# Context tails loaded for two batches at once, a first tile transposed in two halves, and two steps set in another order

## The chip, the core and the metric

The kernel runs on one NeuronCore of one Trainium2 chip. The core has five engines with instruction queues of their own: PE (TensorE, matrix products and transposes through an identity matrix), DVE (VectorE), ACT (ScalarE), POOL (GpSimd) and SP (SyncE, which here only issues DMA transfers). Sixteen DMA engines move data between the chip's memory (HBM) and the core's working memory (SBUF); PE writes to eight accumulator banks (PSUM). The metric is the device time of one execution, in microseconds.

## What is computed

A block of three layers on `x` (8 batches of 64 rows, width 512), each behind a layer norm and added to `x`. All data is 32-bit floating point. The layer that the change touches most is the first, cross-attention from 64 rows of `x` to 1601 context rows per batch:

```python
qp = q @ Wq + bq
kp = k @ Wk + bk
vp = v @ Wv + bv
attn = softmax(qp @ kp.T / sqrt(512))     # k = v = ctx_1024, 1601 rows per batch
x = x + attn @ vp                          # q = layernorm(x)
...
x = x + attn_layer(layernorm(x))           # 16 heads of 32, sigmoid instead of softmax, gates
...
x = x + ffn(layernorm(x))                  # 8 experts, the best one per row
```

## The kernel before

The 512 rows of `x` are four tiles (0 to 3) of 128 rows; a tile holds two batches. For cross-attention the kernel never forms keys: it multiplies a tile's projected queries by Wk transposed (`keyed`), and takes the scores against the context itself. The values likewise: the probabilities multiply the context (`attend`), and the sum is projected by Wv afterwards (`at_out`). So each tile needs the 1601 context rows of its two batches twice: as they are, and transposed.

**Loads.** A batch's first 1536 rows come in three chunks of 1 MB (`load_group`, groups 0 to 2, issued at L216), the last 65 rows as a "tail" (group 3, L223): four loads of 17, 16, 16 and 16 rows that go to partitions 0, 32, 64 and 96 of a tile of their own, `tails[k][b2]`, two buffers for two batches. POOL clears these four tiles first (L205); the second and later of its memsets stand behind the one that begins the identity matrix, and the first stands between that matrix's two instructions. All large loads are issued by SP in program order unless the scheduler moves them: the first tile of `x`, half of Wq, the other three tiles of `x`, the other half of Wq, WkT in halves, then for tile 0 the chunks of groups 0, 1, 2 for both batches and the eight tail loads. An issue waits until the load eight places before it has landed, because eight completion semaphores go round.

**Transposes of the context.** DVE turns blocks of 32x32 (L245 for a chunk, L252 for a tail): `turn_group(T, p, q, b2, g)` makes group `g` of quarter `q` of the width for batch `b2` of tile `p`. For tile 0 seven of the eight blocks `T` are turned group by group as the chunks land (`turn_first`), the eighth, (3, 1), behind them.

**Order.** PE runs in exactly the program's order all through the kernel (a manual schedule); DVE and ACT do so in the first part, up to the scores of tile 0, and in some later stretches. The first part on PE is: idle transposes of the identity, the transposes of the first normalized tile (`turn_x(0)`, L179; one bank, copied to SBUF by ACT in two halves, L304), two idle transposes, `project_q` of tile 0 (L315, which goes through the four chunks of width in order), transposes of tiles 1 and 2, `keyed(0)`, `project_q` of tiles 1 to 3, the scores of quarter 0 of tile 0 over the first 256 columns (`scores(..., hi=256)`), a bias product (L379), the same scores over the remaining columns (`scores(..., lo=256)`, which need groups 2 and 3 of both batches), then quarters 1 to 3 (all L411).

After the scores of a tile follow its softmax on DVE and ACT (exponentials at L433 and L439), transposes of the probabilities (`chance`, L457), and `attend`. For tiles 1 to 3 the Wv projection of the tile before (`at_out`, L187 and the sum at L485) is issued with `chance` as a step between its two halves:

```python
            at_out(p - 1, chance)
            if p == 1:
                keep_keyed(NT - 1, qk)
```

The second layer and the experts are written as a list of named steps whose order is PE's order. Near the end one such list has `flip(0)` (transposes of the first sorted rows, L179, copied by ACT at L1087; the rows were written to memory by POOL and come back by a load that SP issues at L1083), `split(2)` (transposes of queries and keys of tile 2, copied by ACT and DVE, L561 and L563) and `up_first(0)` (the first expert product, L1097, which needs the copy that `flip(0)` makes).

Of the kernel before, what the change touches and what calls it, by code (L numbers as in the profile page):

```python
# [10 lines left out]
F32 = mybir.dt.float32  # L11
# [6 lines left out]
P = 128  # L18
B, S, D = 8, 64, 512
SK = 1601  # L20
NT = B * S // P
DC = D // P
# [14 lines left out]
def perceiver_kernel(ctx: ExitStack, tc: tile.TileContext, out: bass.AP, t: dict):  # L37
# [13 lines left out]
    def slab(name):  # L51
        return slabs.tile([P, DC, D], F32, tag="slab", name=name)
# [10 lines left out]
    def bank4(name):  # L63
        return banks.tile([P, DC, P], F32, tag="bank", name=name)
# [8 lines left out]
    def load_x(i, n):  # L73
        rows = t["x"].rearrange("(i p) d -> p i d", p=P)
        nc.sync.dma_start(out=xall[:, i : i + n, :], in_=rows[:, i : i + n, :])
# [8 lines left out]
    for dc in (0, 2):  # L84
        nc.sync.dma_start(out=wq[:, dc : dc + 2, :], in_=t["xWq"][:, dc : dc + 2, :])
        if dc == 0:
            for i in range(1, NT):
                load_x(i, 1)
    wkT = slab("w_xWkT")
    for dc in (0, 2):  # L90
        nc.sync.dma_start(out=wkT[:, dc : dc + 2, :], in_=t["xWkT"][:, dc : dc + 2, :])
# [84 lines left out]
    def transposed(src, name):  # L176
        tp = bank4(f"t_{name}")
        for dc in range(DC):
            nc.tensor.transpose(tp[:, dc, :], src[:, dc * P : (dc + 1) * P], ident)  # L179
        return tp  # L180

    def projected(srcT, w, name, between=None):
# [14 lines left out]

    scale = 1.0 / math.sqrt(D)
    tails = [
        [one.tile([P, D], F32, tag=f"tail{k}{b2}", name=f"tail{k}{b2}") for b2 in range(2)]  # L200
        for k in range(2)
    ]
    for k in range(2):
        for b2 in range(2):
            nc.gpsimd.memset(tails[k][b2], 0.0)  # L205


    REST = (17, 16, 16, 16)
    def load_group(p, g):
        got = []  # L210
        for b2 in range(2):
            src = t["ctx"][2 * p + b2]
            if g < 3:
                c = slab(f"cx_{p}_{g}_{b2}")
                rows = src[: 12 * P, :].rearrange("(q c) d -> q c d", c=12)
                ins = nc.sync.dma_start(out=c, in_=rows[:, 4 * g : 4 * g + 4, :])  # L216
                if p == 1 and g == 0:
                    tc.keep_in_program_order(ins)
            else:
                c = tails[p % 2][b2]  # L220
                k0 = 12 * P
                for a, n in enumerate(REST):
                    ins = nc.sync.dma_start(  # L223
                        out=c[32 * a : 32 * a + n, :], in_=src[k0 : k0 + n, :]
                    )
                    if p < 2:
                        tc.keep_in_program_order(ins)
                    k0 += n
            got.append(c)
        return got  # L230

    cxs = {}
    for g in (0, 1, 2, 3):
        cxs[0, g] = load_group(0, g)


    NB = D // 32
# [60 lines left out]
        return xns  # L298

    def turn_x(i, xn):  # L300
        tp = transposed(xn, f"xn{i}")
        step = 2 if i == 0 else DC
        for dc in range(0, DC, step):
            nc.scalar.copy(  # L304
                xnT[:, dc : dc + step, i * P : (i + 1) * P], tp[:, dc : dc + step, :]
            )

    def project_q(i0, n, ps):

# [19 lines left out]
        T = slabs.tile([P, DC, D], F32, tag="slab", name=f"T_0_{q}_{b2}")  # L329
        first[q, b2] = T[:, :, :416]  # L330

    def turn_first(g, qs=range(4)):
        for b2 in range(2):
            for q in qs:
                if (q, b2) in first:
                    turn_group(first[q, b2], 0, q, b2, g)
# [29 lines left out]
    def keep_keyed(p, ps):  # L366
        n = len(ps)
        for k in range(n):
            qkTs[p + k] = row4(f"qkT{p + k}")
            for h in range(n):  # L370
                w = DC // n
                nc.scalar.copy(qkTs[p + k][:, h * w : h * w + w, :], ps[h][:, :, k, :])
# [521 lines left out]
    def at_out(i, between=None):  # L894
        project(i, tile_of[i]["acT"], between)
# [15 lines left out]
    def do(*steps):  # L911
        for f, i in steps:
            f(i)
# [29 lines left out]
            for q in qs:  # L943
                turn_group(second[q, b2], 1, q, b2, g)

    for qs in (range(2), range(2, 4)):
        for g in (2, 3):
            turn_first(g, qs)
    scores(0, 0, R, sc, [first[0, 0], first[0, 1]], lo=256)
    first[3, 1] = blocks(0, 3, 1)  # L950
    for q in range(1, 4):
# [7 lines left out]
    for p in range(NT):  # L959
        i = p - 2  # L960
        if p > 0:
            sc = [bank(f"sc_{p}_{a}") for a in range(4)]
        for q in range(4) if p > 0 else ():
            if p == 1 and q == 0:
                nTs = [second[1, 0], second[1, 1]]
            elif p == 1 and q == 1:
                turn_second(2, (2,), (0,))
                nTs = [second[2, 0], blocks(1, 2, 1)]
                turns.__exit__(None, None, None)
            else:  # L970
                nTs = quarter(p, q + 1) if q < 3 else None
            if i >= 0 and q == 3:
                scores(p, q, R, sc, Ts, range(3))
                do((back, i))
                scores(p, q, R, sc, Ts, (3,))
            else:
                scores(p, q, R, sc, Ts)
            Ts = nTs
            if i >= 0 and q < 3:
                do(((split, align, sums)[q], i))  # L980
        if p > 0:
            do((at_turn, p - 1))
        if p == 0:
            turns = tc.manual_schedule(engines={mybir.EngineType.DVE})
            turns.__enter__()
        L, over_sum = softmax(p, sc)
        pts = []
        if p == 0:
            second = {(q, b2): block_tile(1, q, b2) for q in range(2) for b2 in range(2)}
            for g in (0, 1, 3):  # L990
                turn_second(g)
        r = over_sum()
        acts = ExitStack()
        if p < NT - 1:
            acts.enter_context(tc.manual_schedule(engines={mybir.EngineType.Activation}))

        def chance():
            pts.append(chances(p, len(pts), L))

        if p == 0:  # L1000
            qk = keyed(1, 2)
        else:
            if i >= 0:
                do((output, i))
        if p == 0:
            chance()
            tables()
            keep_keyed(1, qk)
            R = queries(1)
        elif p + 1 < NT:  # L1010
            R = queries(p + 1)
            if p == 1:
                qk = keyed(NT - 1)
            at_out(p - 1, chance)
            if p == 1:
                keep_keyed(NT - 1, qk)
        else:
            at_out(p - 1, chance)
        if 0 < p < NT - 1:
            load_pair(p + 1)  # L1020
        if p == 1:
            blank_rows()
        ac = bank(f"ac_{p}")
        if i >= 0:
            do((face, i))
        for g in range(4):
            if g < 3:
                chance()
            if p == 0 and g == 3:
                turn_second(2, (0,), (0,))  # L1030
                second[2, 0] = block_tile(1, 2, 0)
                for gg in (0, 3, 1):
                    turn_second(gg, (2,), (0,))
            if p > 0 and g == 3:
                do((turn, p - 1))
            if 0 < p < NT - 1 and g > 0:
                deal_queries(R, qkTs[p + 1], g, range(2))
                deal_queries(R, qkTs[p + 1], g, range(2, 4), nc.gpsimd.tensor_copy)
            if i >= 0 and g == 1:
                do((gated, i))  # L1040
            if 0 < p < NT - 1 and g == 0:
                deal_queries(R, qkTs[p + 1], 0, range(2))
                deal_queries(R, qkTs[p + 1], 0, range(2, 4), nc.gpsimd.tensor_copy)
            attend(p, g, pts[g], ac)
            if p == 0 and g < 3:
                deal_queries(R, qkTs[p + 1], g)
                if g == 2:
                    deal_queries(R, qkTs[p + 1], 3)
            if p > 0 and g == 0:
                do((norm, p - 1))  # L1050
            if i >= 0 and g == 0:
                do((logits, i))
            if i >= 0 and g == 1:
                do((routed, i))
        if p == 0:
            turn_second(2, (0,), (1,))
        tile_of[p]["acs"] = divided(p, ac, r)
        if p == 0:
            turn_second(2, (1,))
        if 0 < p < NT - 1:  # L1060
            do((unit_q, p - 1))
        acts.close()
        if 0 < p < NT - 1:
            Ts = quarter(p + 1, 0)
            do((unit_k, p - 1), (gates, p - 1), (values, p - 1))
        elif p == 0:
            Ts = [second[0, 0], second[0, 1]]
# [78 lines left out]
    fetch(0)  # L1146
    load_experts_late(gu, dn)
    do((unit_q, 2), (at_turn, 3), (unit_k, 2), (at_out, 3), (norm, 3), (gates, 2))
    do((values, 2), (flip, 0), (split, 2), (up_first, 0), (turn, 3), (align, 2), (up_last, 0))
    do((unit_q, 3), (over, 0), (sums, 2))  # L1150
    unit_k(3, lambda: back(2))
    do((flip, 1), (output, 2))
# [134 lines left out]
```

## Time and profile before

| | us |
|---|---|
| three runs | 288.61, 288.14, 286.54 (median 288.14) |
| the profiled execution | 286.62 |
| its span, first to last instruction | 284.7 |
| PE idle at the start, up to the first idle transpose | 1.86 |
| PE idle from 30 to 33 us, two waits for DVE | 2.3 |
| DVE waiting for context chunks up to 70 us, seven waits | 14.4 |
| SP held in the tail issues of tile 0, first to last issue | 18.4 |
| mean of one chunk transpose on DVE (128x512) | 0.68 |
| DMA traffic, whole span | 57.72 MB, mean 203 GB/s |

The profile is one execution recorded by the hardware profiler. In its timeline a row is: start in us from the beginning of the span, duration, engine, line of the kernel, operation, the tile written and the tiles read, the shape, how many instructions are merged, and in brackets how long the engine stood idle before and what released it. PEld is the weight load of TensorE, SPq a transfer being issued by SyncE. The granted TensorE clock is full in all forty slices of the page. The trace also holds a record for each DMA packet and for each completion that a transfer posts; the prediction calls the latter landing records.

The waits that SP's queue had in the first 35 us, longest in total first:

```profile
SPq L223 <- DMA cx<-in_ctx_dram: 14.9, 6, 3.4
SPq L216 <- DVE T L252: 3.5, 1, 3.5
SPq L223 <- DMA w_xWkT<-in_xWkT_dram: 1.8, 2, 0.9
```

### The profile page before, as it was taken

The numbers are of one execution on the slowest core, as the hardware profiler recorded it, in microseconds if no ns is written. First come the engines' busy times: TensorE is split into PE (matmuls) and PEld (weight loads), VectorE is DVE, ScalarE is ACT, GpSimd is POOL, SyncE is SP. The second block draws the span as 40 slices with busy tenths as digits, with TensorE's granted clock in tenths as the row PEclk, the third lists the DMA queues.
The fourth block names the chain that finished last, engine by engine and source line by source line (L and its number), as shares of the span: only waits on it lengthen the run. The fifth ranks groups of instructions, "written<-read, shape, count | busy, mean of one in ns | idle before, by whom it ended". The sixth has DMA issues, their size and how long they took to land. (4 is left out here: it accounts for less than half of the span.)

```text
span 284.7 us, 6695 instructions
## 1 busy us (share of the span) xinstructions
PE 270.7 (95%) x2724; PEld 136.0 (48%) x2724; DVE 159.1 (56%) x422; ACT 113.4 (40%) x244; POOL 70.5 (25%) x120
## 2 busy tenths in 40 slices
PE   6999699999999999999999999999999999999990
PEld 5975548335643345644434564434444555442320
DVE  3576729359432987846688765631562476384130
ACT  2574006980176522267744047534326424130210
POOL 3351560000971004060220400031140041404211
PEclk9999999999999999999999999999999999999999
DMA  6997686399799980000897036299980200614501
GB/s 210 423 416 308 196 290 236 92 423 395 265 316 397 383 321 9 6 0 0 315 361 284 2 146 211 92 294 367 359 309 2 76 0 2 211 48 149 151 0 45
DMA packets 20177, 57.72 MB, mean 203 GB/s; under 512 B 2418, under 2 KB 10658, under 8 KB 16432
## 3 DMA queue, kind: packets, MB, share of 16 engines
q1 hardware_dynamic: 17568, 50.37, 48.2%
q0 software_dynamic: 2432, 6.89, 6.9%
q8 instruction: 23, 0.38, 0.6%
q14 instruction: 10, 0.08, 0.1%
q10 hardware_dynamic: 144, 0.00, 0.0%
HBM read 50.94 MB, written 6.84 MB: 203 GB/s over the span
## 5 line engine op out<-in xcount | busy, mean ns | idle before, releaser
L245 DVE STREAM_TRANSPOSE T<-cx 128x512 f32<-128x512 f32 x96 | 61.5, 678 | 19.0 <-DMA cx<-in_ctx_dram 18.6
L411 PE MATMUL sc<-T,R 32*64 32x400 f32 (+4 forms) x1088 | 48.1, 480 | 2.4 <-DVE T L252 2.3
L467 PE MATMUL ac<-cx,pt 128*64 128x512 f32 x192 | 43.8, 598 | 0.1
L411 PEld LDWEIGHTS sc<-T,R 32*64 32x64 f32 x1088 | 24.1, 131 | 21.0 <-issue 14.6
L401 ACT COPY R<-qkT 32x512 f32<-32x512 f32 x40 | 24.6, 616 | 0.7
L467 PEld LDWEIGHTS ac<-cx,pt 128*64 128x64 f32 x192 | 12.7, 136 | 22.2 <-issue 21.4
L1097 PE MATMUL gu<-wgu,xeT 128*32 128x512 f32 x192 | 22.8, 597 | 0.0
L544 POOL TENSOR_TENSOR gm_k<-qn_k,c_gk 128x512 f32<-128x512 f32 x4 | 5.1, 1282 | 60.0 <-DVE qn_k L539 60.0
L401 POOL COPY R<-qkT 32x512 f32<-32x512 f32 x24 | 14.5, 605 | 17.4 <-PE sc L411 10.9
L422 DVE TENSOR_REDUCE mx<-sc 128x1 f32<-128x400 f32 (+1 forms) x16 | 8.1, 568 | 13.5 <-PE sc L411 13.5
L187 PE MATMUL p_po<-w_xWv,acT 128*128 128x512 f32 x32 | 14.9, 592 | 0.0
L359 PE MATMUL qk<-qpT,w_xWkT 128*128 128x128 f32 (+1 forms) x96 | 14.8, 311 | 0.0
L187 PE MATMUL p_q<-w_aWq,xhT 128*128 128x512 f32 x32 | 14.8, 606 | 0.0
L187 PE MATMUL p_k<-w_aWk,xhT 128*128 128x512 f32 x32 | 14.7, 595 | 0.0
L315 PE MATMUL qp<-xnT,w_xWq 128*128 128x128 f32 (+1 forms) x64 | 14.5, 383 | 0.1
L187 PE MATMUL p_o<-w_aWo,cT 128*128 128x512 f32 x32 | 14.5, 596 | 0.0
L187 PE MATMUL p_v<-w_aWv,xvT 128*128 128x512 f32 x32 | 14.4, 592 | 0.0
L507 POOL TENSOR_TENSOR x<-x,c_bo 128x512 f32<-128x512 f32 x4 | 5.1, 1273 | 36.3 <-DVE xh L506 36.3
L359 PEld LDWEIGHTS qk<-qpT,w_xWkT 128*128 128x128 f32 x96 | 13.4, 191 | 1.4 <-issue 0.6
L459 ACT COPY pt<-pp 128x512 f32<-128x512 f32 (+1 forms) x16 | 8.2, 510 | 10.4 <-PE pp L457 10.3
L315 PEld LDWEIGHTS qp<-xnT,w_xWq 128*128 128x128 f32 x64 | 9.7, 191 | 4.5 <-ACT xnT L304 0.4
L1132 PE MATMUL y<-wd,hT 128*32 128x512 f32 x96 | 11.5, 596 | 0.3 <-ACT hT L1124 0.3
(197 smaller groups left out, 371.3 us busy)
## 6 DMA issues: line engine op xcount, KB each, us to landing
cx<-in_ctx_dram SPq DMA_DIRECT2D x24, 1024.0 KB, 8.5
wgu<-in_wgT_dram SPq DMA_DIRECT2D x8, 512.0 KB, 9.9
wgu<-in_wuT_dram SPq DMA_DIRECT2D x8, 512.0 KB, 7.1
wd<-in_wdT_dram SPq DMA_DIRECT2D x8, 512.0 KB
rd<-blank POOLq DMA_DIRECT2D x6, 258.0 KB, 6.1
in<-rd SPq DMA_DIRECT2D x6, 258.0 KB, 4.2
xd<-blank POOLq DMA_DIRECT2D x6, 256.0 KB, 5.8
in<-xd SPq DMA_DIRECT2D x6, 256.0 KB, 7.1
```

Of the source, the lines that this page charges most:

```text
L187: nc.tensor.matmul(ps, lhsT=srcT[:, dc, :], rhs=w[:, dc, :], start=(dc == 0), stop=(dc == DC - 1),)
L245: nc.vector.transpose(T[:, :, 128 * g : 128 * g + 128].rearrange("p b (c k) -> p b c k", k=32), cxs[p, g][b2][:, :, 128 * q : 128 * q + 12 ...
L315: nc.tensor.matmul(ps[ec][:, : n * P], lhsT=wq[:, dc, ec * P : (ec + 1) * P], rhs=xnT[:, dc, cols], start=(dc == 0), stop=(dc == DC - 1),)
L359: nc.tensor.matmul(ps[c * n // DC][:, c % (DC // n), :, :], lhsT=wkT[:, ec, c * P : (c + 1) * P], rhs=qpT[:, ec, cols], start=(ec == 0), s ...
L401: copy(R[32 * a : 32 * a + 32, j::4, :], qkT[32 * j : 32 * j + 32, :, :])
L411: nc.tensor.matmul(sc[a][r : r + S, lo : min(hi, WIDTH[a])], lhsT=R[32 * a : 32 * a + 32, b, r : r + S], rhs=Ts[b2][32 * a : 32 * a + 32, ...
L422: nc.vector.tensor_reduce(mx[:, a : a + 1], sc[a][:, : WIDTH[a]], AX.X, ALU.max)
L459: nc.scalar.copy(pt[:, :nch, :], tp[:, :nch, :])
L467: nc.tensor.matmul(ac[r : r + S, :], lhsT=pt[:, j, r : r + S], rhs=cx[b2][:, j, :] if g < 3 else cx[b2], start=(g == 0 and j == 0), stop=( ...
L507: nc.gpsimd.tensor_tensor(xs[i], xs[i], bo, ALU.add)
L1097: nc.tensor.matmul(ps[c, :], lhsT=xTs[k][:, dc, c], rhs=ffw[e][0][:, dc, :], start=(dc == 0), stop=(dc == DC - 1),)
L1132: nc.tensor.matmul(y[c, :], lhsT=hT[:, ic, c], rhs=ffw[e][1][:, ic, :], start=(ic == 0), stop=(ic == IC - 1),)
```

## The change

- The tails of two batches share one tile of 2x512 columns per partition, `tails[k]`, and come in four loads per tile of `x` instead of eight: each of the four takes its 17 or 16 rows of both batches. POOL's four memsets become two of twice the width.
- For tile 0 the four tail loads are issued before the last chunk (group 2, second batch) instead of behind it. DVE's later `turn_first` steps follow that order.
- The fourth tile of `x` is loaded behind the second half of Wq.
- The first tile's four transposes go to two banks, two each; ACT copies the first half, DVE the second.
- For tile 2, `chance` comes behind `at_out` and no longer between its halves. Tiles 1 and 3 keep the step between.
- `split(2)` comes before `flip(0)`.

```diff
-            for i in range(1, NT):
-                load_x(i, 1)
+            load_x(1, 1)
+            load_x(2, 1)
+    load_x(3, 1)
...
     tails = [
-        [one.tile([P, D], F32, tag=f"tail{k}{b2}", name=f"tail{k}{b2}") for b2 in range(2)]
-        for k in range(2)
+        one.tile([P, 2, D], F32, tag=f"tail{k}", name=f"tail{k}") for k in range(2)
     ]
...
+    def load_tails(p):
+
+        c = tails[p % 2]
+        k0 = 12 * P
+        for a, n in enumerate(REST):
+            ins = nc.sync.dma_start(
+                out=c[32 * a : 32 * a + n, :, :],
+                in_=t["ctx"][2 * p : 2 * p + 2, k0 : k0 + n, :].rearrange("b r d -> r b d"),
+            )
+            if p < 2:
+                tc.keep_in_program_order(ins)
+            k0 += n
+        return [c[:, b2, :] for b2 in range(2)]
...
-    for g in (0, 1, 2, 3):
+    for g in (0, 1):
         cxs[0, g] = load_group(0, g)
+    cxs[0, 2] = [load_chunks(0, 2, 0)]
+    cxs[0, 3] = load_group(0, 3)
+    cxs[0, 2].append(load_chunks(0, 2, 1))
...
     def turn_x(i, xn):
-        tp = transposed(xn, f"xn{i}")
-        step = 2 if i == 0 else DC
-        for dc in range(0, DC, step):
-            nc.scalar.copy(
-                xnT[:, dc : dc + step, i * P : (i + 1) * P], tp[:, dc : dc + step, :]
-            )
+        cols = slice(i * P, (i + 1) * P)
+        if i > 0:
+            nc.scalar.copy(xnT[:, :, cols], transposed(xn, f"xn{i}"))
+            return
+
+        for h, copy in enumerate((nc.scalar.copy, nc.vector.tensor_copy)):
+            tp = bank4(f"t_xn{i}_{h}")
+            for dc in (2 * h, 2 * h + 1):
+                nc.tensor.transpose(tp[:, dc, :], xn[:, dc * P : (dc + 1) * P], ident)
+            copy(xnT[:, 2 * h : 2 * h + 2, cols], tp[:, 2 * h : 2 * h + 2, :])
...
-    for qs in (range(2), range(2, 4)):
-        for g in (2, 3):
-            turn_first(g, qs)
+    turn_first(2, range(3), (0,))
+    turn_first(3, range(2))
+    turn_first(2, range(3), (1,))
+    turn_first(3, (2,))
+    for g in (2, 3):
+        turn_first(g, (3,))
...
-            at_out(p - 1, chance)
             if p == 1:
+                at_out(p - 1, chance)
                 keep_keyed(NT - 1, qk)
+            else:
+                at_out(p - 1)
+                chance()
...
-    do((values, 2), (flip, 0), (split, 2), (up_first, 0), (turn, 3), (align, 2), (up_last, 0))
+    do((values, 2), (split, 2), (flip, 0), (up_first, 0), (turn, 3), (align, 2), (up_last, 0))
```

More of the change, by code (lines that the diff above doesn't have):

```diff
@@ L199, in perceiver_kernel, with load_chunks @@
     tails = [
-        [one.tile([P, D], F32, tag=f"tail{k}{b2}", name=f"tail{k}{b2}") for b2 in range(2)]
-        for k in range(2)
+        one.tile([P, 2, D], F32, tag=f"tail{k}", name=f"tail{k}") for k in range(2)
     ]
     for k in range(2):
-        for b2 in range(2):
-            nc.gpsimd.memset(tails[k][b2], 0.0)
+        nc.gpsimd.memset(tails[k], 0.0)
     REST = (17, 16, 16, 16)
-    def load_group(p, g):
[L210 to L224, printed above, removed]
-                    )
[L226 to L230, printed above, removed]
+    def load_chunks(p, g, b2):
+        c = slab(f"cx_{p}_{g}_{b2}")
+        rows = t["ctx"][2 * p + b2][: 12 * P, :].rearrange("(q c) d -> q c d", c=12)
+        ins = nc.sync.dma_start(out=c, in_=rows[:, 4 * g : 4 * g + 4, :])
+        if p == 1 and g == 0:
+            tc.keep_in_program_order(ins)
+        return c
+    def load_tails(p):
[7 more added lines that the diff above has]
+            if p < 2:
+                tc.keep_in_program_order(ins)
+            k0 += n
+        return [c[:, b2, :] for b2 in range(2)]
+    def load_group(p, g):
+        return [load_chunks(p, g, b2) for b2 in range(2)] if g < 3 else load_tails(p)
     cxs = {}
-    for g in (0, 1, 2, 3):
+    for g in (0, 1):
         cxs[0, g] = load_group(0, g)
+    cxs[0, 2] = [load_chunks(0, 2, 0)]
+    cxs[0, 3] = load_group(0, 3)
+    cxs[0, 2].append(load_chunks(0, 2, 1))
     NB = D // 32
@@ L300, in turn_x @@
     def turn_x(i, xn):
-        tp = transposed(xn, f"xn{i}")
-        step = 2 if i == 0 else DC
-        for dc in range(0, DC, step):
-            nc.scalar.copy(
-                xnT[:, dc : dc + step, i * P : (i + 1) * P], tp[:, dc : dc + step, :]
-            )
+        cols = slice(i * P, (i + 1) * P)
[7 more added lines that the diff above has]
+            copy(xnT[:, 2 * h : 2 * h + 2, cols], tp[:, 2 * h : 2 * h + 2, :])
     def project_q(i0, n, ps):
@@ L330, in perceiver_kernel, with turn_first @@
         first[q, b2] = T[:, :, :416]
-    def turn_first(g, qs=range(4)):
-        for b2 in range(2):
+    def turn_first(g, qs=range(4), batches=range(2)):
+        for b2 in batches:
             for q in qs:
```

## The prediction

> **What bounds the kernel now.** The page's first part comes first: one engine fills the span.
>
> ```profile
> PE 270.7 (95%) x2724; PEld 136.0 (48%) x2724; DVE 159.1 (56%) x422; ACT 113.4 (40%) x244; POOL 70.5 (25%) x120
> ```
>
> PE is idle for 284.7 - 270.7 = 14.0 us; its timeline ends at 276.27 + 1.92 = 278.2, so 6.5 us of that is the last scatter behind it, and 7.5 us is all that a reordering can take back. The chain of waits helps little (it names only the last scatter), so the second view is the list of waits, for PE alone:
>
> ```profile
> PE sc L411 <- DVE T L252: 2.3, 2, 1.5
> PE idle L120 <- POOL ident masks.py:199: 1.9, 1, 1.9
> PE pp L457 <- ACT L L433: 0.8, 1, 0.8
> PE t_xe L179 <- DMA in<-xd: 0.6, 1, 0.6
> PE t_xn L179 <- DVE xn L288: 0.6, 1, 0.6
> ```
>
> The columns are total, times, longest. Four of these five rows lie at places that the diff touches; the third view, the timeline in order of time, shows each. The largest, around 24 to 33 us:
>
> ```profile
> 25.56 1.30 DVE L245 STREAM_TRANSPOSE T<-cx 128x512 f32<-128x512 f32 x2 [0.59 <-DMA cx<-in_ctx_dram]
> ...
> 28.48 1.08 PE L379 MATMUL qb<-qpT,c_xbk 128*32 128x128 f32 x32
> 28.74 1.31 DVE L245 STREAM_TRANSPOSE T<-cx 128x512 f32<-128x512 f32 x2 [1.88 <-DMA cx<-in_ctx_dram]
> ...
> 30.30 0.46 PE L411 MATMUL sc<-T,R 32*64 32x145 f32 x2 [0.74 <-DVE T L252]
> ...
> 31.90 0.51 DVE L252 STREAM_TRANSPOSE T<-tail 128x128 f32<-128x128 f32 x2 [1.47 <-DMA tail<-in_ctx_dram]
> 32.27 0.80 PEld L411 LDWEIGHTS sc<-T,R 32*64 32x64 f32 x49 [1.78 <-DVE T L252]
> 32.27 1.01 PE L411 MATMUL sc<-T,R 32*64 32x145 f32 x46 [1.52 <-DVE T L252]
> ```
>
> The last big chunk of each batch lands at 25.5 and 28.7; the second batch's tail only at 31.8. PE has done all else by 29.56 and takes up scores(lo=256) at 32.27; from there to 128 us it stands still for 0.2 us in all, so what is won at 32.27 stays won. The other two places, in PE's timeline:
>
> ```profile
> 125.99 1.88 PE L187 MATMUL p_po<-w_xWv,acT 128*128 128x512 f32 x4
> 128.63 0.65 PE L457 MATMUL pp<-ident,L 128*128 128x128 f32 x4 [0.75 <-ACT L L433]
> 129.12 1.88 PE L187 MATMUL p_po<-w_xWv,acT 128*128 128x512 f32 x4
> ```
>
> ```profile
> 209.70 0.63 PE L179 MATMUL t_xe<-ident,in 128*128 128x128 f32 x4 [0.64 <-DMA in<-xd]
> 210.16 0.60 PE L179 MATMUL t_q<-ident,qn_q 128*128 128x128 f32 x4
> 210.60 0.60 PE L179 MATMUL t_k<-ident,qn_k 128*128 128x128 f32 x4
> 211.13 2.06 PE L1097 MATMUL gu<-wgu,xeT 128*32 128x512 f32 x16
> ```
>
> **The change, part by part. First rows in halves.** Now four transposes start 5.88, 6.15, 6.36, 6.57, end 6.99, ACT copies at 7.03 and PE starts project_q at 7.46. With a bank per half ACT can start at the second transpose's end, 6.57, and is done by 6.57 + 0.03 + 0.37 = 6.97; but the two idle turns (6.79 and 7.00, 0.21 apart) stay ahead, so project_q starts at 7.21: 0.25 us. Its 17th matmul now waits for the second half of Wq (landed 9.27; 0.17 and 0.18 instead of 0.11 between starts there); with the fourth x tile behind it, one 0.67 us transfer less (x tiles 2 and 3 landed at 7.31 and 7.98), it lands at 8.6: 0.1 us more, 0.35 in all. DVE pays: its half of the copy (0.41, the row of the 128x256 hT copy) waits for the fourth transpose, so the statistics queued behind go from 6.68 to about 7.45, and xn1 to xn3 are each 0.75 later (9.8, 11.2, 11.9). PE wants xn2 at 11.1: 0.15 lost of the 0.35. POOL's tail memset ahead of the identity is twice as wide (0.53 becomes 0.96 by the 128x128 row, 0.21, and this one), so the idle turns begin at 2.3 instead of 1.86; their 3.2 us still end before xn0 at 5.82. All of this ends in the stall at 29.6 us: PE comes there 0.2 to 0.35 earlier and waits longer. I count it as nothing; if the stall went entirely it would be worth that much.
>
> The spacing of PE's matmuls drops from 213 to 112 ns at 7.7 us, with the idle turns begun at 1.86. The Trainium skill ("TensorE: Matmul & The Clock Gate", Part 1) has full clock after a free-running window of about 3.4 us with PE busy; by that rule a start 0.43 later risks, one time in eight, a further window at half rate, 1.7 us. In this trace the stall would swallow that too (from 29.2 to about 30.9).
>
> **The tails.** SP's eight tail issues now run from 10.6 to 29.05 us, the last held until the last big chunk has landed, 28.7 (eight completion semaphores go round). Afterwards four issues stand before that chunk; what they would wait for (x, WkT, the first chunk) lands by 14.6, and the chunk's own issue waits for one landing at 16.87. So SP is off the path and the DMA engines are on it. The landing records say how: a 16-row tail load leaves sixteen records, a 17-row one two, of which one is immediate; its rows go through one DMA engine, one after another (2 KB rows take 84 ns there, 8 KB rows of the chunks 313 ns). Both batches' 17 rows in one load leave 34 on that engine, and the last chunk's share now queues behind them. That engine finishes the previous chunk between 23.8 and 24.4 (fifteen of sixteen records), then 34 + 6 rows x 0.084 = 3.36, then 8 x 0.313 = 2.50: 29.7 to 30.2. Rows were slower, 149 ns, for half a microsecond around 26.5 when loads met; six such add 0.4, so 29.7 to 30.6, and I take 30.1. A second engine lags by 1.2 us since 16 us (25.54 for that chunk); with 6 rows and 2.50 it is done at 28.6, not last. DVE then needs one transpose, 0.71, and PE 0.06 after it: 30.1 + 0.8 = 30.9 instead of 32.27. **Gain 1.4** (0.9 to 1.8). DVE's reordered transposes fit: the first batch's and all tails' are done by 28.6, and behind the chunk it needs 0.67 for the next block of eight, while PE takes 4 us for scores(lo=256).
>
> The Trainium skill ("DMA: Bandwidth & Descriptors", "Why a DMA increments its semaphore by 16 and not by 1") gives a load the largest number of engines up to 16 that divides its slowest dimension: one for 17 rows, as the records show, and one again for 17x2. By that rule the change makes its one engine's queue longer ahead of the last chunk, and the sum above stands. The same page's rules for kernel authors say to coalesce small transfers since each pays about 2 us; by it four loads fewer would be worth 8 us, but consecutive 16-row loads land 0.17 us apart here, so they cost no such thing.
>
> Later tail loads (tiles 1 to 3) shrink to four issues each as well: PE waits for none of them now, so nothing.
>
> **at_out before chance, tile 2 only.** The pp transposes (L457) stand between two halves of a projection and wait for the exponentials, done about 128.5. Put behind, the second half (1.73 between starts) covers that: p_po runs 125.99 to 129.45, pp then, and the first attend, now at 131.80, comes 128.63 - 127.72 = 0.91 earlier, at 130.9 (0.75 by the idle column: a drain is counted busy). Its pt copy (ACT, 0.59 after pp ends at 130.05) is ready at 130.7: just in time. **Gain 0.8 to 0.9**, 0.7 if the copy is late.
>
> **split before flip.** t_xe waits for a landing at 209.6. Afterwards t_q and t_k (0.88) fill that time, t_xe runs from 209.8 to 210.4; but its copy (ACT, 0.59) had the two as cover, and up_first now waits for it: 210.42 + 0.59 + 0.05 = 211.06 against 211.13. The 0.64 stall becomes one of about 0.65 one step later: **0.1**. Where the landing is later than in this execution, up to 0.9 more. It follows PE: the stream ahead of it starts at 184.03 when PE frees a slab.
>
> Sum: 1.4 + 0.85 + 0.1 = 2.35. The profiled execution took 286.62 (span 284.7 and 1.9 around it), so 284.3 in its terms; it lies 1.5 under the median of the runs (286.54, 288.14, 288.61), and 288.14 - 2.35 = 285.8.
>
> **Rivals.** *Stall gone entirely*: the 34 rows spread over more engines, and the lagging one (28.6) is last: PE restarts at 29.4, gain 2.9, sum 3.8, 284.3. For it: half the issues; against: the two records of a 17-row load. *Given back*: tile 1's last chunk comes no earlier, and PE, which waits 0.19 at 71.87 for a block from it, waits longer there; only the two later parts stay: 0.95, 287.2. For it: DVE is idle 6.0 us before that chunk; against: its load (SP, 53.94) is held by PE's attend, so it moves along. *Slower*: one engine's queue, the 40 rows ahead of the last chunk, at the crowded price. Restart is 24.1 + 40r + 2.5 + 0.8; that equals 32.27 at r = 0.122 us, and eats the other 0.95 too at r = 0.145. At 0.16 (upper rows around 27 us) it is 33.8, 1.5 later, in sum 0.6 slower: 288.7. Against: 84 ns is the rule outside that half microsecond.
>
> **How the numbers follow.** Forecast 0.56, stall gone 0.20, given back 0.16, slower 0.08. The forecast's own bounds are gains of 1.6 (0.9 + 0.7) to 2.8 (1.8 + 0.9 + 0.1), so 285.3 to 286.5; runs differ by 2 us, so about 1 is added either way: 284.0 to 287.5 holds 8 in 10. One per cent, about what a measurement here tells from no change, is 2.9 us: over it lie stall gone and the forecast's upper end with the spread, 0.36; slower by that, 0.04; within, 0.60.
>
> **What would show it.** PE's restart of scores(lo=256) near 30.9 behind a T from cx rather than from tail; project_q at 7.2; no wait at pp of tile 2; t_xe's wait replaced by gu's for xeT. A restart past 32.3 proves the queue of one engine; one at 29.4 the spread; a new PE wait between 33 and 128 us, the giving back.

## The result and the profile after

The changed kernel takes 288.2 us (median of 17 runs, 286.44 to 290.19); the kernel before, run beside it, 286.81 (17 runs, 284.76 to 288.61). The ratio is 1.0064, with a 95% interval of 1.0037 to 1.0091: slower by 0.6%, where 0.8% faster was forecast, and above the top of the range, 287.5. A second set of runs of the same kernel (the fifth experiment) gave 1.0045 (1.0007 to 1.0083). The profiled execution of the changed kernel is the fastest of its 17, 286.44 us with a span of 284.3, so it shows where waits went, but not what a typical run costs.

The page's first part, and then the list of waits for PE (total, times, longest):

```profile
PE 270.9 (95%) x2724; PEld 137.1 (48%) x2724; DVE 159.5 (56%) x423; ACT 112.9 (40%) x243; POOL 70.2 (25%) x118
```

```profile
PE idle L121 <- POOL ident masks.py:199: 2.3, 1, 2.3
PE sc L420 <- DVE T L250: 2.2, 2, 2.0
PE gu L1112 <- ACT xeT L1102: 0.7, 1, 0.7
PE t_c L180 <- DVE cg L626: 0.5, 1, 0.5
PE sc L420 <- DVE T L257: 0.3, 1, 0.3
```

PE is busy for 270.9 us, before for 270.7. The wait at `pp` and the one of t_xe are gone, as forecast, and a new one of 0.7 for xeT has come. But the wait at the scores of tile 0 is not smaller. The timeline around it:

```profile
28.18 1.90 DVE L250 STREAM_TRANSPOSE T<-cx 128x512 f32<-128x512 f32 x3 [2.86 <-DMA cx<-in_ctx_dram]
...
29.01 1.08 PE L388 MATMUL qb<-qpT,c_xbk 128*32 128x128 f32 x32
30.03 0.89 DVE L257 STREAM_TRANSPOSE T<-tail 128x128 f32<-128x128 f32 x4
...
30.40 0.46 PE L420 MATMUL sc<-T,R 32*64 32x145 f32 x2 [0.30 <-DVE T L257]
...
32.09 1.30 DVE L250 STREAM_TRANSPOSE T<-cx 128x512 f32<-128x512 f32 x2 [1.18 <-DMA cx<-in_ctx_dram]
...
32.86 0.38 PE L420 MATMUL sc<-T,R 32*64 32x145 f32 x8 [2.01 <-DVE T L250]
```

PE is through with the bias product at 30.1 and has nothing to do, but for two products, until 32.86. The prediction had 30.9, the kernel before 32.27. The releaser is now a block from `cx`, the last chunk, as forecast. Its landing records run from 28.94 to 32.07, and the second-to-last chunk, which had ended at 25.54, now ends at 28.16. Both are later than in the sum, and not on one DMA engine alone: fifteen of the last chunk's sixteen shares are in at 31.25, where the sum had them at 28.6. The windows of 1 us of the kernel before, and under them those of the changed kernel, show why; the last two columns are the share of time in which the DMA engines were busy and what they moved:

```profile
core 0: us, PE busy (x) PEld busy (x) DVE busy (x) ACT busy (x) POOL busy (x), PEclk, DMA share, GB/s
...
24.00:25.00 1.00, 1.00 (x5) 0.60 (x4) 0.97 (x2) 0.58 (x1) 0.00 (x0) 1.00 1.00 418
25.00:26.00 1.00, 1.00 (x5) 0.60 (x4) 0.44 (x1) 0.00 (x0) 0.00 (x0) 1.00 0.99 408
26.00:27.00 1.00, 1.00 (x18) 0.42 (x25) 0.87 (x2) 0.33 (x1) 0.00 (x0) 1.00 0.70 185
27.00:28.00 1.00, 1.00 (x54) 0.86 (x42) 0.00 (x0) 0.25 (x1) 0.00 (x0) 1.00 0.12 39
```

```profile
24.00:25.00 1.00, 1.00 (x4) 0.57 (x3) 1.00 (x3) 0.37 (x1) 0.00 (x0) 1.00 0.99 211
25.00:26.00 1.00, 1.00 (x4) 0.57 (x3) 0.32 (x1) 0.21 (x1) 0.00 (x0) 1.00 0.96 186
26.00:27.00 1.00, 1.00 (x4) 0.38 (x2) 0.00 (x0) 0.00 (x0) 0.00 (x0) 1.00 1.17 203
27.00:28.00 1.00, 1.00 (x33) 0.79 (x40) 0.00 (x0) 0.58 (x1) 0.00 (x0) 1.00 0.86 207
```

Before, the chunk runs at 418 GB/s until it is through, and only then do the tail rows come, at 185 GB/s and less, with no chunk queued behind them. After, the DMA engines are as busy from 24 to 28 us as they were before from 24 to 26, but move 186 to 211 GB/s: rows and chunk packets run side by side. By the packet records that start from 24 to 28 us, an 8 KB packet of a chunk takes 0.614 us (median; 0.313 before), a 2 KB row 0.172 (0.094 before). In the three other traces of this order of loads (experiments 3, 5 and 10) the 8 KB packets take 0.39 to 0.41 in the same stretch, so 0.614 is the worst of four.

The two late steps, in PE's timeline:

```profile
126.72 3.60 PE L188 MATMUL p_po<-w_xWv,acT 128*128 128x512 f32 x8
130.16 0.60 PE L466 MATMUL pp<-ident,L 128*128 128x128 f32 x4
...
131.56 2.80 PE L476 MATMUL ac<-cx,pt 128*64 128x512 f32 x12
```

```profile
209.09 0.60 PE L180 MATMUL t_k<-ident,qn_k 128*128 128x128 f32 x4
209.52 0.60 PE L180 MATMUL t_xe<-ident,in 128*128 128x128 f32 x4
210.80 2.11 PE L1112 MATMUL gu<-wgu,xeT 128*32 128x512 f32 x16 [0.68 <-ACT xeT L1102]
```

Before, `pp` waited 0.75 between two halves of p_po, and the first attend was this row:

```profile
131.80 3.65 PE L467 MATMUL ac<-cx,pt 128*64 128x512 f32 x16
```

Now the eight products run through and the first attend starts at 131.56, although PE had come to this place 0.73 later (126.72 against 125.99). That is 0.97 won. At 209.52 t_xe no longer waits, and gu waits 0.68 one step later: the trade of 0.1 that was forecast.

In the tables below the mean granted clock of a run is used, since the runs of most kernels fall into two groups by it. Runs far above the others of their kernel are left out, as in the ratios; with them the shares of runs at 0.990 and below in the last table would be 36 of 105 and 22 of 29, and not 30 of 96 and 21 of 28.

### The profile page after: what moved, and what is told of

The parts are those of the page before. It is cut to its first block, busy times and chain, and to the rows that moved or that the text cites. A ratio compares the mean times of both kernels' runs of the same rounds, so it can differ in the third digit from the quotient of the medians.

```text
span 284.3 us, 6663 instructions
## 1 busy us (share of the span) xinstructions
PE 270.9 (95%) x2724; PEld 137.1 (48%) x2724; DVE 159.5 (56%) x423; ACT 112.9 (40%) x243; POOL 70.2 (25%) x118
```

## The experiments

Two theories stood first. **Queue**: the rows of the early tails slow the last two chunks. **Clock**: the longer idle stretch of PE lets its clock drop. A rival was that the late steps cost time. The call `idle_turns(n)`, which some of the kernels add, transposes the identity n times on PE and uses the result nowhere.

**1. Tails behind the last chunk again** (changed kernel, VectorE's order of before).

```diff
-    for g in (0, 1):
+    for g in (0, 1, 2, 3):
         cxs[0, g] = load_group(0, g)
-    cxs[0, 2] = [load_chunks(0, 2, 0)]
-    cxs[0, 3] = load_group(0, 3)
-    cxs[0, 2].append(load_chunks(0, 2, 1))
...
```

> The changed kernel with the four merged tail loads of tile 0 issued behind the last chunk again, and DVE's turn_first steps in the order of before. Theory queue (the 34 rows on one DMA engine, and the crowding while they mix with chunk packets, make the last chunk late: 32.07 us in the changed kernel): the last chunk lands near 28, its packets take 0.31 us again, the tails are in by 30.4 to 31, scores(lo=256) restart at 31.0 to 31.6 instead of 32.86, and the time is 1.3 to 1.8 us under the changed kernel's by that alone. Theory clock (a PE stall of over 2 us in one piece lets the granted clock drop to half for a window of about 3.4 us, at a cost of up to 1.7 us in most executions): the stall is shorter and broken up, the drop becomes rarer, another 0.5 to 1.5 us go. Rival late steps (the loss lies in the p = 2 or flip order): no change against the changed kernel.

Measured: 286.51 us, ratio 0.9985 (0.9945 to 1.0024). The last chunk lands from 26.22 to 29.89 (near 28 was expected), the tails by 31.02, PE restarts at 31.61:

```profile
31.61 5.63 PE L417 MATMUL sc<-T,R 32*64 32x145 f32 x128 [2.35 <-DVE T L254]
```

The loss is gone when the order of loads and of VectorE's transposes goes, so it lies in that order; the restart is still no earlier than 31, since the rows land late instead. (The products take 5.63 us here because the granted clock is at half behind the wait, see below.)

**2. The 17-row load as 16 rows and 1** (changed kernel).

```diff
-        for a, n in enumerate(REST):
...
-                out=c[32 * a : 32 * a + n, :, :],
...
+        for a, n in enumerate(REST):
+            for r0, m in ((0, 16), (16, n - 16)):
+                if m:
...
+                        out=c[32 * a + r0 : 32 * a + r0 + m, :, :],
...
```

> The changed kernel with every 17-row tail load cut in 16 rows and 1 row. Theory queue in its first form (one engine works off 34 rows alone): the tails take half a microsecond on all engines, the last chunk lands at 28.5 to 29, scores(lo=256) restart at 29.4 to 29.8, and the time is 3 us under the changed kernel's, about 1 per cent under before's. In its second form (any 2 KB rows of two batches between chunks slow all engines): chunk packets still take 0.5 us or more and the last chunk lands after 30.5. Rival late steps: no change.

Measured: 285.46 us, 0.9969 (0.9932 to 1.0006). No engine has 34 rows now. The last chunk still lands only at 31.19 and PE restarts at 31.98: 0.88 earlier than in the changed kernel, 1.1 later than the prediction's 30.9. So the long run of rows on one engine is a part, but the slow packets are there without it (8 KB packets at 0.68 to 0.95 us, the medians of the half microseconds from 23.5 to 26.5).

**3. Twenty turns of the identity in the stall** (changed kernel, which otherwise stays).

```diff
     qbT = biased()
+    idle_turns(20)
```

> The changed kernel with twenty idle transposes on PE between the bias product and scores(lo=256), that is 2.2 us of work in the stall from 30.1 to 32.9; nothing else. Theory clock: mean granted clock of the runs goes up from 0.982 to 0.992 towards 0.994, and the median falls by 1 to 1.7 us; the profiled restart stays at 32.9. Theory queue alone: the same time as the changed kernel, within 0.3 us, and the same clocks. Rival late steps: no change.

Measured: 287.0 us, 1.0013 (0.9974 to 1.0051). The clock of the runs is 0.990 to 0.998, where that of the changed kernel is 0.982 to 0.994. PE restarts at 33.53, later than ever, since the chunk's last share lands at 32.74, and by the medians the kernel is still 0.4% faster than the changed one (287.0 / 288.2). The intervals of the two ratios overlap, so the time alone does not show it; with the clocks of the runs it speaks for a part of the loss being the clock.

**4. The two late edits alone, on the kernel before** (the last two parts of the change's diff).

> The kernel before with only the two late edits: chance behind at_out for tile 2, and split before flip. Theories queue and clock: 0.7 to 1.0 us faster than before (ratio about 0.997), PE's wait at pp gone, its wait for xeT in place of the one for the load. Rival late steps: slower than before by 1 us or more.

Measured: 285.55 us, 0.9963 (0.9924 to 1.0002). The rival falls: these two edits do not cost.

**5. The changed kernel once more.**

> The changed kernel itself, unchanged, to see an execution near its median and its mean granted clock on the same chip as the next three. Clock theory: its profiled execution, or most of its runs, shows a half-rate window of 3.41 us that covers the restart of scores(lo=256) near 32.8 us, mean clock at or below 0.990 in more than half of the runs (the kernel before: 12 of 35 in the runs beside the first four experiments), and runs with that clock are 1 to 2 us longer than runs above it. Rival (the loss lies in the loads alone): the median is above that of the kernel before also among runs with a mean clock above 0.992, by 0.5 us or more.

Measured: 288.13 us, 1.0045 (1.0007 to 1.0083); 7 of 11 runs at a clock of 0.990 or less, median 288.24; the three at 0.993 have 286.28. The rival has a share too, by three runs only: they are 0.6 above the runs of the kernel before at that clock (285.68). The profiled execution, at 290.23 the longest of the twelve, restarts where the first profile did, and loses its clock there:

```profile
32.86 6.58 PE L420 MATMUL sc<-T,R 32*64 32x145 f32 x126 [2.08 <-DVE T L250]
```

The trace's clock records have half rate from 31.50 to 38.33, and the products that took 3.96 take 6.58: 2.62 of the 3.79 us between the two executions, with the restart the same.

**6. Twelve turns in the stall of the kernel before.**

```diff
     qbT = biased()
+    idle_turns(12)
```

> The kernel before with 12 turns of the identity on TensorE behind qbT = biased(), so in its own stall of 0.74 + 1.52 us; 12 at the 0.12 us each that 20 of them took in the third experiment (2.40 us) are 1.4 us and end ahead of the restart at 32.3. Nothing else differs. Clock theory: no half-rate window behind warm-up in the profile, mean clock above 0.990 in nearly all runs, the upper part of the kernel before's times (287 to 289) is missing; median 285.0 to 285.6, 0.4 to 0.7% below the kernel before. Rival (the clock's drop costs nothing, since the stall swallows it, as the prediction had it): median as before, 286.8 within 0.3%.

Measured: 286.9 us, 1.0019 (0.999 to 1.0048). The first half held: no run at or below 0.990. The second did not: the time did not fall. The 128 products of 401 columns take 6.23 us instead of 5.63 (see experiment 8); what else is lost stays open. By the clock records of the profiled execution the full clock begins at 10.82 us, not at 7.07, and the bias product 1.4 us later than before, and yet the scores go on at 32.38 (32.27 before).

**7. The order of the loads alone, with eight separate tail loads** (kernel before).

```diff
-    for g in (0, 1, 2, 3):
+    for g in (0, 1):
         cxs[0, g] = load_group(0, g)
+    cxs[0, 2] = load_group(0, 2, (0,))
+    cxs[0, 3] = load_group(0, 3)
+    cxs[0, 2] += load_group(0, 2, (1,))
...
```

> The kernel before with the order of the loads alone: the first pair's eight separate tail loads (one batch each) stand ahead of the last chunk, with the transposes of the changed kernel's order on VectorE; the first rows, fourth tile and late steps as before. Theory queue, first form (2 KB rows that run beside 8 KB packets slow all engines, whoever issues them): 8 KB packets take 0.5 us or more between 24 and 28 us, the last chunk lands at 31.5 to 32.3, restart of scores(lo=256) at 32.3 to 33.0, median 287 to 288.5. Rival merge (the slow rows come from the two-batch form, whose one load reads from two places and writes both halves of a partition): 8 KB packets stay near 0.31 us, the last chunk lands by 30.5, restart by 31.2, and the median is 1 us or more below the kernel before.

Measured: 287.39 us, 1.0015 (0.9983 to 1.0047), restart at 32.76. Restart and median lie in the ranges of theory queue, but SP's timeline shows another reason.

```profile
7.98 0.33 SPq L216 DMA_DIRECT2D cx<-in_ctx_dram  x1
9.33 17.37 SPq L223 DMA_DIRECT2D tail<-in_ctx_dram  x8
26.74 6.42 SPq L216 DMA_DIRECT2D cx<-in_ctx_dram  x3
```

The eight issues hold SP for 17.37 us, because each waits for the load eight places before it, so the last chunk is issued at 26.74 and the DMA engines move 29 to 84 GB/s between 24 and 27 us. The run says nothing of crowding, but it says what the merging was good for: with four loads that chunk is issued at 17.96.

**8. The late edits and the twelve turns.**

> The two late edits alone (split before flip; at_out before chance in the second tile) with the same 12 turns of the identity in the stall: a candidate against both kernels. Clock theory with the late steps worth about 1 us: mean clock above 0.990 in nearly all runs, median 284.2 to 284.8, 0.7 to 0.9% below the kernel before, and about 1 us below the kernel before with the turns alone. Rival (the turns only take the place of an idle window that mostly does no harm): as the fourth experiment, 285.5, in two groups 2 us apart.

Measured: 285.97 us, 0.9966 (0.9943 to 0.999), all 12 runs at 0.993 or above. That is 1.3 over the runs of experiment 4 at such a clock (284.69). Not all of it need be the price of the turns: runs that keep their clock without turns may be those whose stall happened to be short (experiment 11), and no run here tells the two apart. PE's timeline:

```profile
29.52 1.53 PE L120 MATMUL idle<-ident 128*128 128x128 f32 x12
...
32.37 3.96 PE L411 MATMUL sc<-T,R 32*64 32x145 f32 x126 [0.93 <-DVE T L252]
...
36.52 6.04 PE L411 MATMUL sc<-T,R 32*64 32x401 f32 x128
```

The turns end well ahead of the restart, but later the 128 products of 401 columns take 6.04 us, where they take 5.63 in the kernel before (36.42 to 41.98) and in the changed one. In experiment 6 it is 6.23, in experiment 11 it is 6.30. In these traces all of the extra time lies in the last sixteen of the 128 products, in experiment 9 in the same place, and the profile names no wait there. A pause ahead does not tell them apart: 0.93 us here, none in experiment 6, but 0.82 in experiment 3, whose products take 5.63. Why TensorE issues slower there stays open.

**9. No tails for the first two batches** (changed kernel; it leaves out 130 context rows, so it is no candidate).

```diff
-        for a, n in enumerate(REST):
+        for a, n in enumerate(REST if p else ()):
```

> The changed kernel without the four tail loads of the first pair of batches (p = 0; the tiles keep the zeros of the memset, so the last 65 context rows of two batches are left out). All chunk loads, transposes and matmuls stay. Theory queue (the rows slow the chunk packets that run beside them): 8 KB packets stay near 0.31 us to the end, the pair of chunks of g = 2 lands by 25.6 and 26.8 instead of 28.2 and 32.1, the transposes of the last chunk are no longer waited for, scores(lo=256) starts right behind the bias (30.1 to 30.3) and runs through with less than 0.5 us of waiting, so restart 2 us or more earlier than 32.86 and no half-rate window there; median 284.0 to 285.5. Rival (the last chunk is late for another reason: the issue on SP, the pool's slab, or the chunk's own bytes): it lands after 29 as well, and the restart stays within 0.7 us of 32.86.

Measured: 284.42 us, 0.991 (0.9874 to 0.9946). Its windows and PE's timeline:

```profile
24.00:25.00 1.00, 1.00 (x5) 0.60 (x4) 1.00 (x3) 0.58 (x1) 0.00 (x0) 1.00 1.03 426
25.00:26.00 1.00, 1.00 (x4) 0.59 (x4) 0.41 (x2) 0.00 (x0) 0.00 (x0) 1.00 0.93 385
```

```profile
28.45 1.08 PE L388 MATMUL qb<-qpT,c_xbk 128*32 128x128 f32 x32
29.46 3.98 PE L420 MATMUL sc<-T,R 32*64 32x145 f32 x128
...
33.63 5.60 PE L420 MATMUL sc<-T,R 32*64 32x401 f32 x120
39.94 0.90 PE L420 MATMUL sc<-T,R 32*64 32x400 f32 x8 [0.70 <-issue]
```

The 8 KB packets that start from 24 to 28 us take 0.313 us (median; nine in ten at most 0.320), the two chunks land by 25.87 and 28.35, and PE goes from the bias product straight on at 29.46. So it is the 130 rows, a fourth of a megabyte, that make the last chunk late: theory queue holds. Of the 3.4 us between 29.46 and 32.86 a part is given back: at 39.94 PE stands 0.70 us with no releaser that the profile knows, the same place of the program as in experiments 6, 8 and 11.

**10. The changed kernel without its two late edits.**

> The changed kernel with its two late steps put back (flip before split, at_out before chance in every tile): the loads, the transposes' order and the halves of the first rows stay. With the fourth experiment it splits the change in two. If the parts add: the late steps alone were worth 1.0 to 1.2 us (between runs without a half-rate window), so this one is slower than the changed kernel by that, near 289.2, 0.6 to 1.0% above the kernel before, with half-rate windows in more than half of the runs. Rival (the late steps' gain is given back in the changed kernel, by a later wait): no longer than the changed kernel, 288.2 within 0.3%.

Measured: 287.8 us, 1.0073 (1.0041 to 1.0105), 8 of 12 runs at a clock of 0.990 or less. The ratio is where adding the parts puts it, the time is not (289.2 was expected); the median is not above the changed kernel's, so from this run alone the rival is not excluded. Its profiled execution has the clock drop that the changed kernel's lacks. PE's timeline, and the windows around it (PEclk, the granted clock, is the third column from the right):

```profile
30.05 0.46 PE L420 MATMUL sc<-T,R 32*64 32x145 f32 x2 [0.86 <-DVE T L257]
32.62 5.66 PE L420 MATMUL sc<-T,R 32*64 32x145 f32 x126 [2.12 <-DVE T L250]
```

```profile
32.00:33.00 1.00, 0.38 (x24) 0.38 (x32) 1.00 (x2) 0.00 (x0) 1.00 (x3) 1.00 0.87 352
33.00:34.00 1.00, 1.00 (x65) 0.98 (x55) 1.00 (x4) 0.00 (x0) 1.00 (x2) 0.97 1.08 451
34.00:35.00 1.00, 1.00 (x24) 0.88 (x15) 1.00 (x4) 0.00 (x0) 0.03 (x1) 0.50 0.98 287
35.00:36.00 1.00, 1.00 (x20) 0.92 (x13) 1.00 (x3) 0.00 (x0) 0.00 (x0) 0.50 0.91 217
36.00:37.00 1.00, 1.00 (x23) 0.88 (x15) 0.90 (x2) 0.00 (x0) 0.00 (x0) 0.50 0.97 377
37.00:38.00 1.00, 1.00 (x27) 0.54 (x12) 0.00 (x0) 0.00 (x0) 0.04 (x1) 0.83 1.03 409
```

PE restarts at 32.62 behind a gap of 2.12 us; from 33.93 to 37.35 (the trace's clock records; 3.41 us) the clock is at 0.5. The 126 products that took 3.96 at full clock take 5.66: 1.70 more.

**11. The late edits and six turns.**

> The two late edits on the kernel before and only six turns of the identity in the stall (0.7 us, where twelve took 1.53 us). Clock theory with an account of idle time per window: TensorE is left with 1.4 to 1.5 us of idle in the stall, below the 1.8 us at which windows at half rate were seen, so nearly no run shows one and the median is 284.6 to 285.2. Rival (the turns themselves cost the 1.3 us by which the kernel with twelve stood above the runs of the fourth experiment without a half-rate window): 285.2 to 286.0 with no half-rate windows, in proportion to their number or not.

Measured: 285.54 us, 0.9981 (0.9946 to 1.0017); 3 of 12 runs still at 0.990 or less, the other nine 285.43. Both expectations miss a part. The profiled execution restarts at 30.71, as its tails landed by 30.52 (31.78 in the kernel before): the stall of the old order can differ by 1.5 us between executions. The four other traces of that order (before, 4, 6 and 8) restart at 32.24 to 32.38.

**12. Merged tails behind the last chunk, 16 and 1 rows, six turns** (changed kernel with the edits of 1, 2 and 3).

> A candidate: the changed kernel with its two-batch tail loads set behind the last chunk and VectorE's order of before (first experiment), 17 rows split as 16 and 1 (second), and six turns of the identity in the stall. Theory queue: no chunk packet waits behind rows of the same batches' tails, the last chunk lands by 30, the tails by 30.6, restart of scores(lo=256) by 31.6; theory clock: mean clock above 0.990 in nearly all runs. Median 284.0 to 284.8, below the first, second and fourth experiments. Rival: the tails behind the chunk land later than 31 and the restart is at 32.3 again; then 284.7 to 285.5.

Measured: 284.75 us, 0.9943 (0.9911 to 0.9974), all 12 runs at 0.993 or above.

```profile
29.25 0.87 PE L121 MATMUL idle<-ident 128*128 128x128 f32 x6
31.55 4.34 PE L421 MATMUL sc<-T,R 32*64 32x145 f32 x128 [1.43 <-DVE T L258]
...
36.09 5.63 PE L421 MATMUL sc<-T,R 32*64 32x401 f32 x128
```

PE restarts at 31.55 and the 128 products of 401 columns take 5.63. The last chunk lands by 29.98 and the tails by 30.67, so the restart is as expected, and the time lies where the ranges of the expectation and of its rival overlap. This version beats both kernels: 0.6% below the kernel before, 1.2% below the changed one by the ratio of medians (284.75 / 288.2).

## Why the prediction was wrong

The runs sorted by mean granted clock; the few between 0.990 and 0.993 are counted under "all" only:

| kernel | all: runs, median | 0.993 and above | 0.990 and below |
|---|---|---|---|
| before (three sets) | 96, 286.59 | 54, 285.68 | 30, 287.59 |
| changed (two sets) | 28, 288.19 | 4, 286.36 | 21, 288.20 |
| 4, late edits alone | 12, 285.55 | 7, 284.69 | 5, 287.19 |
| 10, loads and halves alone | 12, 287.80 | 1, 286.75 | 8, 288.00 |
| 3, changed with turns | 12, 287.00 | 10, 286.80 | 2, 288.55 |
| 12 | 12, 284.75 | 12, 284.75 | 0 |

The mean clock is a rough sign of a loss in the stall, since it also counts a half-rate window behind the last product (in the changed kernel's profile from 280.84 to the end). At 0.992 the profile of experiment 1 has the drop and that of experiment 6 has not.

- **The tails: the mechanism was right, the price of a row was not; this term failed first.** The prediction put 40 rows on one DMA engine ahead of that engine's share of the last chunk, at 84 ns each (3.36 us), and allowed the higher price for six. In the trace of after that load lands at 29.14; from the 24.1 of the sum that is 5.0 us for 40 rows, 0.126 us each, an estimate, and the chunk's share then takes 2.9 instead of 2.5 (to 32.07). With the 0.8 of DVE and PE behind it this is 32.86. In experiments 3, 5 and 10 the same load lands at 28.95 to 29.77 and the share takes 2.9 to 3.0 again; this share is the last of the sixteen in all four. The rejected rival had the break-even at 0.122. What the profile of before had shown for half a microsecond (0.149) was not an exception: in the four traces where rows met chunk packets for longer, the median row from 24 to 28 us took 0.109 to 0.172; before, no chunk was queued behind the rows. And the term was laid on one engine, while all are slowed (the fifteen other shares, experiment 2, and experiment 9 with the rows gone). So a gain of 1.4 became a loss of 0.6 in the profiled execution. That the rival's 288.7 lies near the measured time is partly luck: a loss of 0.6 here and the 0.95 of the late steps would still be 0.35 faster, and what made the kernel slower stands under the next point and the last, which the rival did not have either.
- **The stall taken as free time: this step fell too.** The prediction weighed a window at half clock at the start only, and said that the stall would swallow it; that is what experiment 6 shows. What it put at nothing is that the stall itself can make the clock drop, and that this window covers the work behind it, which is on the path (1.70 us in experiment 10). The share of runs at 0.990 and below goes from 30 of 96 to 21 of 28; the two groups of these two kernels lie 1.8 to 1.9 us apart, so by this estimate it is (0.75 - 0.31) x 1.85 = 0.8 us of the 1.6 between the medians. The other 0.7 is the difference between the upper groups (286.36 and 285.68, the first of only four runs). That the turns of experiment 3 leave 2 of 12 runs in the low group, with a later restart, and that twelve turns (experiments 6 and 8) leave none of 24, shows that the idle time is the cause.
- **at_out before chance, 0.8 to 0.9, and split before flip, 0.1: right.** 0.97 in the profile, 0.7 waited one step later, and experiment 4 has 285.68 - 284.69 = 1.0 between the groups at 0.993 and above. It was not enough: in the same groups the loads and halves cost 286.36 - 284.69 = 1.7.
- **First rows in halves, counted as nothing: not contradicted, and not tried alone.** In after, PE starts at 2.28 and waits 0.29 for the second half of Wq, which lands at 9.42 and not at 8.6; both lie ahead of the stall. The bias product starts at 28.11 to 28.25 in five of the eight traces that have the halves, and at 28.45 to 28.57 in four of the six that do not, near the 0.2 to 0.35 that were forecast.
- **The base of the sum.** The profiled execution before restarts at 32.27; experiment 11, with the same order of loads, did so at 30.71. The former kept its clock, and at 286.62 lies 0.9 above the median of such runs (285.68), so part of the stall that the sum meant to win was probably not there in a typical one. And the sum was taken off the median of three runs, 288.14, where that of 17 is 286.81: from there the forecast would have been 284.5, and the miss 3.7 us and not 2.4.

The Trainium skill ("TensorE: Matmul & The Clock Gate", Part 1) gives a free-running window of 3413 ns and the low clock "after ≥1 idle window (~3.4µs)". The length agrees (3.413 us in experiment 10's records), and so does the free run: in the six traces with a drop (1, 2, 4, 5, 7 and 10) the clock falls 7 or 8 whole windows of 3.413 us behind the first record of full clock. The amount of idle time does not agree. Laid on this grid, TensorE's waits in the window just ahead of the fall are 1.72 to 2.22 us; in the eight traces without a drop no window around the stall holds more than 1.43. In the changed kernel's first profile the waits of 0.30 and 2.01 fall into two windows, 1.12 in one and 1.19 in the next; in experiment 5, with the restart at the same 32.86, 1.72 fall into one. So how a stall of this length lies to the windows is luck; the kernels whose wait was gone or at 1.43 in their profiles (9 and 12) lose the clock in none of 24 runs. It is not one threshold for all work: behind the last products of the program three traces (before, 1 and 3) have 1.86 to 2.00 us idle in a window and keep the clock in the next.

## What to carry to other kernels

A transfer moved ahead of another is not paid by its bytes at the quiet price: look in the trace for a moment where the two kinds meet, take the price from there, and apply it to both, and to all engines. A stall of TensorE is not free time: two microseconds of it cost 1.7 more when the clock falls behind it, so the time lost grows in a step, and a profile of one lucky execution doesn't show it. Judge by the runs' clocks as well as by the profile.

## What was not expected of the hardware

- Small packets beside large ones: 130 rows of 2 KB halve the rate of all 16 DMA engines for some 4 us in the changed kernel's first profile (418 to about 200 GB/s, the engines busy throughout), and an 8 KB packet takes 0.614 us instead of 0.313. In experiments 3, 5 and 10 it is some 2 us, at 174 to 289 GB/s. The runs show that it goes with the rows; what in the memory makes it is open.
- The step in the clock: 3.41 us at half rate, 1.70 us in the trace and 1.8 to 1.9 between the groups of runs, behind 1.72 to 2.22 us of waiting in one window.
- Filling a stall may have a price: with twelve turns no run lost the clock, but the kernel was 1.3 us above the runs that kept it without turns. Of this the profile shows 0.4: PE issued slower, with no wait, in the last sixteen of 128 products. Experiments 8 and 9 show that with and without turns, so the turns themselves are not the cause; what TensorE lacks there stays open.
